# Four-head attention's second head pair added inside the first mixture's first pass, and the joins around the mixture and the entries of the next stages rewritten

## The chip, the cores and the metric

The kernel runs on one core of a Trainium2 chip. The core's engines are TensorE (PE, with its weight loads shown apart as PEld), VectorE (DVE), ScalarE (ACT), GpSimd (POOL) and SyncE (SP), which here only issues transfers. The metric is the time of one execution on the device in microseconds (us), less being better. Everything is computed in float32.

## The reference

The program is a graph network of four layers over 2708 nodes with 256 features, and a 2708 x 2708 adjacency matrix. Each layer adds two results to x, each computed from a layer norm of x. What the change touches, shortened:

```python
# layer 1: attention with 4 heads of 64, then a mixture of 8 experts, top 1
h = (x @ W).reshape(n, 4, 64)
e = leaky_relu(si[:, None, :] + sj[None, :, :], 0.2)      # si, sj: scores of h
att = softmax(where(adj > 0, e, NEG), axis=1)
out = einsum('ijh,jhd->ihd', att, h)

H = gelu(xf @ W1 + b1)                                     # 256 -> 1024
probs = softmax(H @ Wg + bg);  assign = argmax(probs)      # 8 experts
for e in range(8):
    out += where(assign == e, probs[:, e] * (H @ Wd[e] + bd[e]), 0)

# layer 2: attention with one head (Wh = h @ W_w + W_b), then decoder
#          attention and 8 experts (682 hidden, gated), top 2
# layer 3: attention with one head and elu, then a linear layer
```

Layer 0 (a cosine graph attention and a slice attention) is not changed, but for a root that it shares with others. With the reference's inputs the first mixture sends 324, 259, 370, 225, 370, 529, 221 and 410 rows to its eight experts, which fill 25 tiles of 128 rows; the second sends 5416 rows, which fill 47.

## The kernel before

The rows of x stay in on-chip memory as X, 22 tiles of 128 rows (the last has 20). Row tiles are grouped in six blocks of 512 columns (the last has 148). A tile framework gives every instruction its semaphores and sets the order on each engine from the program's order, from when it expects operands to be ready, and from explicit constraints (`issue_after`).

*Four-head attention* (`gat_heads`, from line 762) goes over the heads in two pairs. For each of 22 source tiles j, ScalarE and VectorE form the unnormalised weights e (L668, L669); TensorE multiplies them into six accumulators `acc` of 512 columns (L774), then into `den` (L782), which collects the sums for normalisation. At a pair's end `den` is copied, transposed and inverted (L792 to L800). Then each `acc` is copied to `o`, transposed (L809), multiplied by the reciprocals (L816) and added to X (L823).

*The first mixture* (`top1_ffn`, L850) has two passes. Its eight expert matrices `wd` (8 MB) are loaded on SP's queue (L876), into memory that attention gives back at its end. The statistics for the layer norm follow (L144, L145: sums; L146: a root on ScalarE; L149: its reciprocal on VectorE). The first pass goes over the six blocks: `features` normalises and transposes, `hidden` does 16 matmuls of 512 columns (L905) and a Gelu, `gate` computes the router's logits (L931, L937) and each row's place, and scatters row numbers to lists per expert (L1372); `store` transposes the hidden rows back (L920) and stores them (L924), 512 KB a tile. The order is features of the next block, gate, store.

`route.finish` works out, for every tile of the second pass, which expert it belongs to and where its list starts. The second pass goes over 26 "usual" tiles (a conditional branch, not taken with these inputs, would do more): `fetch` loads a tile's 128 row numbers with a row register on SP (L1474), casts them (L962) and gathers the hidden rows (L964); `transposes` (L978, L979) turns them; `results` does 16 matmul instructions with `wd[expert]`, the expert's number being read to a register of TensorE (L985), and two for the bias `bd` (L988), copies (L992, alternately VectorE and ScalarE) and scatters the rows (L1495). Between the first fetches and the first results stand `route.owners`, `route.weights` and `Head`, which loads the next attention's weights on GpSimd's queue and folds its score vectors into them on VectorE (L651, L654).

*Single-head attention* (`gat_single`, used for layer 2 as g2 and layer 3 as g3) first combines the mixture's rows into X (L1526), takes statistics, normalises (L108), transposes (L1098), and projects (L123) by blocks; `parts` sums the transposed features (L1114); ScalarE makes the exponentials and half of the weighted V (L1111), VectorE the other half (L1113). With a bias, 22 GpSimd additions (L1149) put it into X. The main loop is over destination chunks and 22 source tiles j (L1168).

*The experts of layer 2* (top 2, hidden width 682 in two parts) use the same routing with 47 tiles: `fetch` (L1474, row register), `front` (transposes and place), `hidden` (L1794), `results` (L1826).

Lines of the page, such as L876, are lines of this kernel. What the diff touches:

Of the kernel before, what the change touches and what calls it, by code (L numbers as in the profile page):

```python
# [8 lines left out]
F32 = mybir.dt.float32  # L9
# [21 lines left out]
def slot_tiles(choices, experts=8):  # L31

    return (choices * N + experts * (P - 1)) // P
# [19 lines left out]
class Net:  # L53
# [29 lines left out]
    def load_rows(self, pool, ap, n, name, parts=P):  # L83

        t = pool.tile([parts, n], F32, name=name)
        self.nc.gpsimd.dma_start(t, ap.partition_broadcast(parts))
        return t
# [17 lines left out]
    def normed(self, out, t, ln):  # L105
        mean, rstd = ln
        r = rows(t)
        self.nc.vector.tensor_scalar(  # L108
            out[:r], self.X[:r, t, :], mean[:r, t : t + 1], rstd[:r, t : t + 1], ALU.subtract, ALU.mult
        )  # L110
# [15 lines left out]
class Stats:  # L126
# [9 lines left out]
    def sums(self, t0, t1):  # L136
        net, nc = self.net, self.net.nc
        g = slice(t0, t1)
        if t1 == NT:
            nc.vector.memset(self.mv[:, g, :], 1.0)  # L140
        for t in range(t0, t1):
            r = rows(t)
            st = net.stats.tile([P, 6], F32, name="bnst")
            nc.vector.bn_stats(st[:r], net.X[:r, t, :])  # L144
            nc.vector.bn_aggr(self.mv[:r, t, :], st[:r])  # L145
        nc.scalar.activation(self.sd[:, g], self.mv[:, g, 1], AF.Sqrt, bias=net.ln_eps)  # L146

    def roots(self, t0, t1):
        self.net.nc.vector.reciprocal(self.rstd[:, t0:t1], self.sd[:, t0:t1])  # L149
# [151 lines left out]
def inverse_root(net, pool, v, scale, eps, name):  # L301
# [8 lines left out]
    y = pool.tile([P, n], F32, name=f"{name}y")  # L310
    nc.vector.tensor_scalar(y.bitcast(I32), half, -1.0, float(0x5F3759DF), ALU.mult, ALU.add)
    t = pool.tile([P, n], F32, name=f"{name}t")
    for _ in range(4):
        nc.vector.scalar_tensor_tensor(t, y, -0.5, y, ALU.mult, ALU.mult)
        nc.vector.tensor_tensor(t, t, x, ALU.mult)
        nc.vector.scalar_tensor_tensor(y, t, 1.5, y, ALU.add, ALU.mult)
    return y
# [340 lines left out]
def gat_pairs(net, e, j, i0, iw, big_p, ratio):  # L658
# [10 lines left out]
    nc.vector.scalar_tensor_tensor(v, v, 1.0, net.mask[:, j, i], ALU.add, ALU.mult)  # L669


def gat_heads(net):
# [8 lines left out]
    Q = len(cols) // 2  # L681
    with ExitStack() as ctx:
        big = ctx.enter_context(tc.tile_pool(name="g1big", bufs=1))
        V = big.tile([P, NT, H, DH], F32, name="V")
        ratio = big.tile([P, NT, H], F32, name="ratio")

        low = big.tile([P, NT, H, 2 * Q - 1], F32, name="low")
        big_p = big.tile([P, H, N], F32, name="big_p")
# [73 lines left out]
        for p in range(2):  # L762
# [4 lines left out]
            for j in range(NT):  # L767
# [3 lines left out]
                for n, (i0, iw) in enumerate(cols):  # L771
                    for k, h in enumerate(heads):
                        half = slice(k * DH, (k + 1) * DH)
                        nc.tensor.matmul(  # L774
                            acc[n][half, :iw], V[:, j, h, :], e[:, k, i0 : i0 + iw], start=j == 0, stop=j == NT - 1
                        )
# [13 lines left out]

# [5 lines left out]
            rd = small.tile([P, 4, 4, Q], F32, name="rd", bufs=1)  # L796
# [4 lines left out]
            out = []  # L801
            for n, (i0, iw) in enumerate(cols):
                o = small.tile([P, 512], F32, name="o", bufs=3)
                (nc.vector.tensor_copy if n % 2 else nc.scalar.copy)(o[:, :iw], acc[n][:, :iw])
                pt = paux.tile([P, 4, P], F32, name="aux")
                its = tiles_of(i0, iw)
                for c, i in enumerate(its):
                    r = rows(i)
                    nc.tensor.transpose(pt[:r, c, :], o[:, c * P : c * P + r], net.ident)  # L809
                whole = [c for c, i in enumerate(its) if rows(i) == P]  # L810
                for c0, c1, r in [(0, len(whole), P)] + [(c, c + 1, rows(its[c])) for c in range(len(whole), len(its))]:
                    nt = c1 - c0
                    y = small.tile([P, 4, 2, DH], F32, name="y")

                    d = rd.rearrange("p c (k b) q -> p c k b q", b=2)[:r, c0:c1, :, n // Q, n % Q]
                    nc.vector.tensor_tensor(  # L816
                        y[:r, :nt],
                        pt[:r, c0:c1, :].rearrange("p c (k d) -> p c k d", d=DH),
                        d.unsqueeze(3).to_broadcast([r, nt, 2, DH]),
                        ALU.mult,  # L820
                    )
                    xs = X[:r, its[0] + c0 : its[0] + c1, p * 2 * DH : (p + 1) * 2 * DH]
                    nc.vector.tensor_tensor(xs, xs, y[:r, :nt].rearrange("p c k d -> p c (k d)"), ALU.add)  # L823
# [27 lines left out]
def top1_ffn(net, ctx):  # L851

    nc, tc, a, X = net.nc, net.tc, net.a, net.X
    E, HID = 8, 1024
    KC = HID // P
    with ExitStack() as inner:
        big = ctx.enter_context(tc.tile_pool(name="f1big", bufs=1))
        dram = ctx.enter_context(tc.tile_pool(name="f1dram", bufs=1, space=bass.MemoryType.DRAM))  # L860
        wd = inner.enter_context(tc.tile_pool(name="f1wd", bufs=1, side="right")).tile([P, E, KC, D], F32, name="wd")
# [11 lines left out]
        bd = big.tile([E, D], F32, name="bd")  # L873
        nc.gpsimd.dma_start(bd, a["f1_bd"])
        for e in range(E):
            nc.sync.dma_start(wd[:, e], a["f1_wd"][e].rearrange("(c p) m -> p c m", p=P))  # L876
        route = Routing(net, big, dram, 1, "f")
        ln = net.ln_stats()
# [3 lines left out]
        with tc.tile_pool(name="f1tp", bufs=2, space=PSUM) as ptp, tc.tile_pool(  # L882
# [7 lines left out]
            def features(its):  # L890
                ft = work.tile([P, 2, 512], F32, name="ft")
                for k, t in enumerate(its):
                    r = rows(t)
                    f = rp.tile([P, D], F32, name="f", bufs=2)
                    net.normed(f, t, ln)
# [3 lines left out]

            def hidden(ft, nw):  # L900
                halves = [work.tile([P, KC // 2, 512], F32, name="ht", bufs=3) for _ in range(2)]
# [10 lines left out]
            def store(its, halves):  # L912

                for k, t in enumerate(its):
                    r = rows(t)
                    hr = rp.tile([P, 2, 512], F32, name="hr", bufs=2)
                    for n, half in enumerate(halves):
                        ps = pg.tile([P, 4, P], F32, name=f"hr{n}")
                        for c in range(KC // 2):
                            nc.tensor.transpose(ps[:r, c, :], half[:, c, k * P : k * P + r], net.ident)  # L920
                        (nc.scalar.copy if n else nc.vector.tensor_copy)(
                            hr[:r, n, :], ps[:r].rearrange("p c m -> p (c m)")
                        )
                    nc.sync.dma_start(rows_of[span(t), :], hr[:r].rearrange("p n m -> p (n m)"))  # L924

            def gate(its, halves, nw):
# [5 lines left out]
                q4 = rp.tile([P, 512], F32, name="q4", bufs=1)  # L932
# [9 lines left out]
            blocks = chunks(512)  # L942
            ft = features(tiles_of(*blocks[0]))
            for n, (n0, nw) in enumerate(blocks):
                its = tiles_of(n0, nw)
                halves = hidden(ft, nw)
                if n + 1 < len(blocks):
                    ft = features(tiles_of(*blocks[n + 1]))
                gate(its, halves, nw)
                store(its, halves)  # L950
        route.finish()
        prep = ctx.enter_context(tc.tile_pool(name="g2prep", bufs=1))
        with tc.tile_pool(name="f1t", bufs=1, space=PSUM) as pt, tc.tile_pool(
            name="f1y", bufs=2, space=PSUM
        ) as py, tc.tile_pool(name="f1s", bufs=3) as sp:
            held = {}

            def fetch(s):
                node = sp.tile([P, 1], F32, name="node", bufs=6)
                route.load(s, node)  # L960
                number = sp.tile([P, 1], I32, name="number", bufs=6)
                nc.vector.tensor_copy(number, node)  # L962
                hr = sp.tile([P, 2, 4, P], F32, name="hr", bufs=5)
# [4 lines left out]
                    in_offset=bass.IndirectOffsetOnAxis(ap=number, axis=0),  # L968
                )
                held[s] = hr, node  # L970

            def transposes(s):
                hr, node = held.pop(s)
# [6 lines left out]
                return ht, route.where(sp, s, node)  # L980

            def results(s, ht, to):
                ps = py.tile([P, D], F32, name="y")
                for c in range(KC):
                    nc.tensor.matmul(  # L985
                        ps, ht[:, c // 4, c % 4, :], wd[:, bass.ds(experts[s], 1), c, :], start=c == 0, stop=False
                    )
                last = nc.tensor.matmul(  # L988
                    ps, route.hot[:E, s : s + 1].to_broadcast([E, P]), bd, start=False, stop=True
                )  # L990
                y = sp.tile([P, D], F32, name="ys")
                (nc.scalar.copy if s % 2 else nc.vector.tensor_copy)(y, ps)  # L992
                route.send(to, y)
                return last

            experts = {}

            def through(s0, s1, prepare=None):
                last = None
                for s in range(s0, min(s0 + 4, s1)):  # L1000
                    fetch(s)
                    if prepare and s == s0:
                        route.owners()
                ready = transposes(s0)
                if prepare:
                    prepare()
                for s in range(s0, s1):
                    with tc.issue_after(last.ins) if last else nullcontext():
                        experts[s] = nc.tensor.value_load(route.expert[0:1, s : s + 1], min_val=0, max_val=E - 1)
# [3 lines left out]
                    last = results(s, *this)  # L1013
# [3 lines left out]
            heads = []  # L1017

            def prepare():
                with tc.tile_pool(name="f1wt", bufs=1) as one:  # L1020
                    route.weights(one)
                    heads.append(Head(net, prep, one, "g2", True))

            through(0, route.usual, prepare)
            with route.others():
                through(route.usual, route.tiles)
# [3 lines left out]
class Head:  # L1030


    def __init__(self, net, pool, work, key, bias):
        nc, a = net.nc, net.a

# [1038 lines left out]
```

## Time and profile before

| | |
|---|---|
| median of three runs | 2925.66 us |
| lowest and highest | 2923.8 and 2935.31 us |
| the profiled execution | 2935.18 us |
| its span (first to last instruction) | 2933.1 us |
| busy: PE, PEld | 2676.8 us (91%), 1633.7 us (56%) |
| busy: DVE, ACT, POOL | 1458.5 us (50%), 1046.9 us (36%), 367.2 us (13%) |
| mean granted clock of TensorE | 0.943 of full speed |

The stages, by the times at which TensorE's work changes: four-head attention's two pairs up to 1070; the first mixture's first pass 1096 to 1214; the second pass from 1240 to 1377; attention g2 to 1672; decoder attention and routing to 2200; the experts to 2600; attention g3 from there to 2899; the linear layer to 2933.

In a timeline row the columns are start, length, engine, line, operation, output and inputs, shapes, count, and in brackets the idle time before it with what ended it. In a row of groups, after the bar: busy time of the group and mean nanoseconds of one; after the next bar: idle time of the engine just ahead of them and what ended it. A line "issue" in a chain is time in which the engine waited for nothing that the profile shows.

### The profile page before, as it was taken

How to read it: one execution, taken by the hardware profiler on the slowest of the kernel's cores; microseconds unless marked ns; L12 is line 12 of the kernel's file. 1: busy time of each engine (PE TensorE's matmuls, PEld its weight loads, DVE VectorE, ACT ScalarE, POOL GpSimd, SP SyncE). 2: the span in 40 equal slices, each digit the busy share in tenths (PEclk: the TensorE clock that was granted, in tenths of full speed). 3: DMA queues.
4: the chain of work that ended last, by engine and by line, in shares of the span. 5: the costliest groups of instructions: out<-in, count | busy, mean ns of one | idle time of the engine just before them, and what ended most of it. 6: DMA issues, size and time to landing. Idle time of an engine off the chain costs nothing.

```text
span 2933.1 us, 33103 instructions
## 1 busy us (share of the span) xinstructions
PE 2676.8 (91%) x11945; PEld 1633.7 (56%) x11945; DVE 1458.5 (50%) x3089; ACT 1046.9 (36%) x1605; POOL 367.2 (13%) x464
## 2 busy tenths in 40 slices
PE   6999989799999979797899899999969999969998
PEld 4667646563333325486688433333336676747885
DVE  7743358344777773422644455465543222245455
ACT  3344433225665633211543223233312221224453
POOL 0000012100000001232200123233321111110002
PEclk9999999698999989899999999899959999989999
DMA  8899210000000023443200100002031101041001
GB/s 297 283 293 312 85 64 1 8 0 1 1 1 1 1 85 133 115 130 103 77 1 1 33 22 17 15 2 89 15 109 33 33 30 33 29 151 40 1 1 39
DMA packets 110323, 196.66 MB, mean 67 GB/s; under 512 B 12154, under 2 KB 71034, under 8 KB 107454
## 3 DMA queue, kind: packets, MB, share of 16 engines
q1 hardware_dynamic: 89816, 147.89, 15.6%
q0 software_dynamic: 13360, 38.73, 4.2%
q10 hardware_dynamic: 6986, 7.91, 0.9%
q8 instruction: 100, 1.64, 0.2%
q14 instruction: 61, 0.50, 0.1%
HBM read 134.78 MB, written 59.71 MB: 66 GB/s over the span
## 4 chain that ended last, share of the span: by engine, by line
PE 74%; DVE 10%; DMA 5%; issue 5%; ACT 3%; POOL 2%; ACTq 0%; POOLq 0%; SPq 0%; DVEq 0%
PE acc L1168 15%; PE acc L774 8%; PE acc L278 7%; PE den L782 4%; PE po L1826 4%; PE po L1656 4%; PE sc L1641 3%; PE score L267 3%; DMA f<-hs 3%; PE h L905 3%; PE h L1794 3%; PE pv L123 2%; PE sc L1619 2%; PE po L123 2%; PE y L985 1%
## 5 line engine op out<-in xcount | busy, mean ns | idle before, releaser
L669 DVE SCALAR_TENSOR_TENSOR e<-e,mask 128x768 f32<-128x768 f32 (+2 forms) x264 | 409.5, 1566 | 312.9 <-ACT e L668 312.7
L668 ACT ACTIVATE e<-big_p,minus_one,ratio 128x768 f32<-128x768 f32 (+2 forms) x264 | 394.8, 1513 | 362.8 <-PE acc L1168 229.4
L1168 PE MATMUL acc<-V,e 128*128 128x257 f32 (+1 forms) x1936 | 433.5, 383 | 4.5 <-DVE e L669 2.8
L1168 PEld LDWEIGHTS acc<-V,e 128*128 128x128 f32 (+1 forms) x1936 | 352.2, 186 | 85.8 <-issue 32.1
L774 PE MATMUL acc<-e,V 128*64 128x512 f32 (+1 forms) x1056 | 249.7, 550 | 4.1 <-DVE e L669 4.1
L1794 PE MATMUL h<-w,ft 128*128 x752 | 233.9, 453 | 0.5 <-ACT ft L1783 0.5
L278 PE MATMUL acc<-F,e 128*128 128x257 f32 x968 | 226.3, 384 | 3.0 <-DVE e L275 2.6
L278 PEld LDWEIGHTS acc<-F,e 128*128 128x128 f32 x968 | 173.4, 185 | 67.0 <-DVE e L275 28.4
L774 PEld LDWEIGHTS acc<-e,V 128*64 128x64 f32 x1056 | 95.4, 137 | 180.6 <-issue 158.1
L1641 PE MATMUL sc<-qt,kt 64*128 64x512 f32 (+4 forms) x656 | 185.7, 538 | 4.3 <-ACT e L1651 2.6
L1651 ACT ACTIVATE e<-sc 128x1024 f32<-128x1024 f32 (+4 forms) x140 | 102.7, 760 | 201.1 <-PE sc L1641 177.7
L1794 PEld LDWEIGHTS h<-w,ft 128*128 128x128 f32 x752 | 136.4, 191 | 56.9 <-issue 1.6
L275 DVE TENSOR_TENSOR e<-e,mask 128x512 f32<-128x512 f32 (+2 forms) x132 | 80.5, 625 | 149.2 <-ACT e L269 147.4
L1659 DVE TENSOR_TENSOR sum<-sum,e 128x1024 f32<-128x1024 f32 (+4 forms) x102 | 104.1, 1020 | 97.7 <-ACT e L1651 94.1
L269 ACT ACTIVATE e<-score 128x512 f32<-128x512 f32 (+2 forms) x132 | 69.7, 544 | 179.8 <-PE score L267 153.1
L1656 PE MATMUL po<-e,V 128*64 128x512 f32 (+5 forms) x560 | 119.1, 509 | 14.9 <-ACT e L1651 8.9
L1826 PE MATMUL po<-w,ht 114*128 x564 | 131.2, 382 | 0.9 <-DVE ht L1819 0.9
L1641 PEld LDWEIGHTS sc<-qt,kt 64*128 64x128 f32 x656 | 71.3, 199 | 95.3 <-issue 81.5
L782 PE MATMUL den<-e,low 128*3 128x512 f32 (+1 forms) x1056 | 123.1, 542 | 0.0
L1826 PEld LDWEIGHTS po<-w,ht 114*128 114x128 f32 x564 | 107.9, 191 | 23.1 <-DVE ht L1819 8.2
L1485 DVE TENSOR_SCALAR second<-f,down 128x1 f32<-128x1 f32 x47 | 9.9, 213 | 219.1 <-DMA f<-hs 219.1
L267 PE MATMUL score<-QK 128*128 128x512 f32 (+2 forms) x264 | 112.8, 558 | 1.2 <-ACT e L269 0.7
(600 smaller groups left out, 3554.8 us busy)
## 6 DMA issues: line engine op xcount, KB each, us to landing
row<-in_adj SPq DMA_DIRECT2D x21, 1354.0 KB
raw<-in_adjT SPq DMA_DIRECT2D x35, 768.0 KB
hs<-zero SPq DMA_DIRECT2D x8, 2838.0 KB
hidden<-hr SPq DMA_DIRECT2D x21, 512.0 KB
wd<-in_f_wd SPq DMA_DIRECT2D x8, 1024.0 KB
kept<-mask SPq DMA_DIRECT2D x21, 338.5 KB
mask<-kept SPq DMA_DIRECT2D x21, 338.5 KB
f<-hs SPq DMA_DIRECT2D x47, 129.0 KB
```

The lines of the kernel that those rows point to most:

```text
L123: self.nc.tensor.matmul(out, lhsT[:, c, :], rhs[:, c, :], start=first and c == 0, stop=last and c == n - 1)
L267: nc.tensor.matmul(ps[:r, :iw], QK[:, 0, span(j)], QK[:, 1, i0 : i0 + iw], start=True, stop=True)
L278: nc.tensor.matmul(acc[k][:ri], e[:r, k * P : k * P + ri], F[:r, j, :], start=j == 0, stop=j == NT - 1)
L668: nc.scalar.activation(v, big_p[:, i], AF.Relu, bias=net.minus_one, scale=ratio)
L669: nc.vector.scalar_tensor_tensor(v, v, 1.0, net.mask[:, j, i], ALU.add, ALU.mult)
L774: nc.tensor.matmul(acc[n][half, :iw], V[:, j, h, :], e[:, k, i0 : i0 + iw], start=j == 0, stop=j == NT - 1)
L782: nc.tensor.matmul(den[g : g + Q, :iw], low[:, j, h, Q - 1 - q : 2 * Q - 1 - q], e[:, k, i0 : i0 + iw], start=False, stop=j == NT - 1 and ...
L1168: nc.tensor.matmul(acc[k][:ri], e[:, k * P : k * P + ri], V[:, j, :], start=j == 0, stop=j == NT - 1)
L1641: nc.tensor.matmul(ps[:r, g, o:iw], kt[b, span(j)], qt[b, o:iw], start=True, stop=True)
L1656: nc.tensor.matmul(po[b, o:iw], V[:r, j, g, :], e[:r, g, o:iw], start=j == 0, stop=j == last)
L1794: last = nc.tensor.matmul(halves[s, n][:, q, :HALF], fts[s][:, c, :], weights.w13[n][:, bass.ds(es[s], 1), c, q * HALF : (q + 1) * HALF], ...
L1826: last = nc.tensor.matmul(po, ht[:KP, k, :], w2[:KP, bass.ds(es[s], 1), k, :], start=k == 0, stop=k == KC - 1)
```

## The change

Seven parts, in the order of the program.

1. `gat_heads` does `den` before `acc` for each source tile. Both pairs' `acc` are copied to a buffer `o` that outlives the function; pair 1 is added to X as before; the adding of pair 2 is returned as a function. `top1_ffn` calls it for blocks 0 to 2 ahead of the first hidden rows and for blocks 3 to 5 after block 0's, with the statistics between, in an order on VectorE given by `turn`. For blocks from 1 on, the root is made on VectorE (`newton`). `wd` is loaded after the last add, into the memory of `o`.
2. The hidden rows are stored by half rows (256 KB each) from a buffer of three, which `q4` shares. The store of block 4 follows gate of block 5.
3. The routing gives each expert one of the first eight tiles, so those need no registers; their row numbers come with one transfer (`load_first`). Row numbers, casts and places are kept for all tiles and made in groups of four. Owners and weights come after the first fetch.
4. In the second pass the bias matmul is gone; the copy of each result becomes a VectorE addition of `bd`, held for all partitions (1 MB) and loaded on ScalarE's queue; for tiles from 8 on the expert's number is also read to a register of VectorE. `Head` loads on ScalarE's queue after tile 3.
5. `gat_single` takes `parts` from the copies themselves (`accum_out`, two copies of half the size), leaves the weighted V of blocks 0 to 3 to ScalarE, orders VectorE's steps with `turn`, and uses `newton` for later blocks. The 22 GpSimd additions of the bias come in the first chunk of the main loop, at j = 3.
6. The experts of layer 2 use fixed numbers for their first eight tiles, and `place` is apart from `front`; owners and shares come after the first gate.
7. `inverse_root` does three iterations in place of four.

The core of the diff:

```diff
 def gat_heads(net, keep):
+    o = keep.tile([P, len(cols), 4 * P], F32, name="o")
+    def add(p, n, psum, tag):
+        pt = psum.tile([P, 4, P], F32, name="aux", tag=tag)
+        for c, i in enumerate(its):
+            nc.tensor.transpose(pt[:r, c, :], o[:, n, c * P : c * P + r], net.ident)
+        ...
+            nc.vector.tensor_tensor(y[:r, c0:c1], pt[...], d..., ALU.mult)
+            last = nc.vector.tensor_tensor(xs, xs, y[...], ALU.add)
+        return last
...
             for n, (i0, iw) in enumerate(cols):
+                (nc.vector.tensor_copy if n % 2 else nc.scalar.copy)(o[:, n, :iw], acc[n][:, :iw])
+                if p == 0:
+                    add(p, n, paux, "aux")
+    return lambda n, psum, tag: add(1, n, psum, tag)
...
 def top1_ffn(net, ctx):
+            turn(add, 0, ptp, "tp")
+            turn(stats.sums, *tiles[0])
+            turn(add, 1, ptp, "tp")
+            turn(stats.roots, *tiles[0])
             ft = features(tiles_of(*blocks[0]))
+            turn(stats.sums, *tiles[1], root=False)
+            turn(add, 2, ptp, "tp")
+            turn(stats.sums, *tiles[2], root=False)
+            turn(stats.newton, rp, tiles[1][0], tiles[2][1])
             for n, (n0, nw) in enumerate(blocks):
                 halves = hidden(ft, nw)
                 if n + 1 < len(blocks):
                     ft = features(tiles_of(*blocks[n + 1]))
+                if n == 0:
+                    for m in range(3, len(blocks)):
+                        turn(add, m, ptp, "tp")
+                        turn(stats.sums, *tiles[m], root=False)
+                    turn(stats.newton, rp, tiles[3][0], NT)
+                    held.close()
+                    for e in range(E):
+                        nc.sync.dma_start(wd[:, e], ...)
                 gate(its, halves, nw)
+                kept.append((its, halves))
+                if n + 2 != len(blocks):
+                    for k in kept:
+                        store(*k)
+                    kept.clear()
...
-                last = nc.tensor.matmul(
-                    ps, route.hot[:E, s : s + 1].to_broadcast([E, P]), bd, start=False, stop=True
-                )
-                (nc.scalar.copy if s % 2 else nc.vector.tensor_copy)(y, ps)
+                        e = expert(nc.vector, s)
+                    added = nc.vector.tensor_tensor(y, ps, bd[:, e, :]..., ALU.add)
...
 def gat_single(net, key, head, feed, elu):
-                    nc.scalar.copy(ft[:, :, k * P : k * P + pw], ps[:, :, :pw])
+                    for c in range(2):
+                        nc.scalar.activation(ft[:, c, ...], ps[:, c, :pw], AF.Copy,
+                            accum_out=parts[:, 2 * n + k // 2, c : c + 1])
-                nc.vector.tensor_reduce(parts[:, n, :], ft[:, :, :nw], AX.X, ALU.add)
-            if bias:
-                for t in range(NT):
-                    nc.gpsimd.tensor_tensor(X[:r, t, :], X[:r, t, :], bias[:r], ALU.add)
...
+                if bias is not None and i0 == 0 and j == 3:
+                    for t in range(NT):
+                        nc.gpsimd.tensor_tensor(X[:r, t, :], X[:r, t, :], late[:r], ALU.add)
...
+    def load_first(self, f):
+        self.loaded = self.net.nc.sync.dma_start(
+            f, self.hs.rearrange("(e c) d -> c (e d)", e=self.E)[:P, :]
+        )
```

## The prediction

> **What bounds the kernel now.** I read the chain of work that ended last first, then the engines' busy time stage by stage, then the timeline and the chain inside the stages that the diff touches. The chain, by engine:
>
> ```profile
> PE 74%; DVE 10%; DMA 5%; issue 5%; ACT 3%; POOL 2%; ACTq 0%; POOLq 0%; SPq 0%; DVEq 0%
> ```
>
> TensorE sets the time wherever it has work; what can be won is where it has none. The next view gives, for each stretch, its length, the busy time of PE, PEld, DVE, ACT and POOL, the granted clock, the DMA share and GB/s:
>
> ```profile
> 1070.00:1096.00 26.00, 9.92 (x37) 5.82 (x38) 23.68 (x93) 3.65 (x8) 4.89 (x13) 0.55 0.60 186
> 1096.00:1214.00 118.00, 118.00 (x542) 64.21 (x541) 43.94 (x164) 43.22 (x69) 17.81 (x19) 0.98 0.35 129
> 1214.00:1240.00 26.00, 4.74 (x28) 3.09 (x26) 15.87 (x79) 2.79 (x4) 9.44 (x11) 0.60 0.52 84
> 1302.00:1442.00 140.00, 116.19 (x534) 87.43 (x532) 61.30 (x151) 40.79 (x106) 42.94 (x50) 0.91 0.35 108
> 2165.00:2200.00 35.00, 11.41 (x44) 5.90 (x44) 18.59 (x92) 2.12 (x7) 9.62 (x14) 0.50 0.59 209
> 2590.00:2679.00 89.00, 55.95 (x214) 39.79 (x212) 49.86 (x142) 31.62 (x88) 5.99 (x7) 0.79 0.44 154
> ```
>
> Row 1 is the end of four-head attention: VectorE full, PE a third. Row 2, the first mixture's first pass, is PE without a gap. Rows 3, 5 and 6 are joins (to the second pass, the experts, the last attention) with PE mostly idle; the second half of row 4 is the join to biased attention.
>
> The timeline around row 1 (start, length, engine, line):
>
> ```profile
> 1066.95 2.75 PE L782 MATMUL den<-e,low 128*3 128x512 f32 x24
> ...
> 1083.84 17.83 SPq L876 DMA_DIRECT2D wd<-in_f_wd  x8
> ...
> 1095.55 5.86 PE L905 MATMUL h<-ft,w 128*128 128x512 f32 x8
> ```
>
> Attention's last matmul ends at 1069.70 (call it S); the mixture's first comes at S+25.8. Between lie six adds, all statistics, the first features. The 8 MB of expert weights start meanwhile and keep the rings full for about 25 us.
>
> The chain through row 3, at its DMAs:
>
> ```profile
> 1223.68 4.20 DMA fnodes<-ftag,fto
> ...
> 1229.55 2.71 DMA g2bv<-in_g_b
> ...
> 1236.35 4.04 DMA hr<-hidden,number
> ```
>
> The second is not the mixture's: the folds of the next attention's head, which wait for their own loads, stand on VectorE ahead of the cast of the first tile's numbers.
>
> One steady tile of the second pass, by timeline:
>
> ```profile
> 1346.52 1.09 PE L978 MATMUL ht<-ident,hr 128*128 128x128 f32 x8
> 1347.45 3.62 PE L985 MATMUL y<-wd,ht 128*128 x16
> ...
> 1351.00 0.69 PE L988 MATMUL y<-bd,fhot 8*128 8x256 f32 x2
> 1351.62 1.09 PE L978 MATMUL ht<-ident,hr 128*128 128x128 f32 x8
> ```
>
> 5.10 us from tile to tile, of which the bias matmul is 1351.62 − 1351.00 = 0.62.
>
> Groups of the join to biased attention (busy, mean ns, idle before):
>
> ```profile
> L1149 POOL TENSOR_TENSOR X<-X,g2bv 128x256 f32<-128x256 f32 x21 | 15.5, 770 | 18.9 <-DVE f L108 18.8
> L108 DVE TENSOR_SCALAR f<-X,mv,rstd 128x256 f32<-128x256 f32 x21 | 14.2, 737 | 0.0
> L1114 DVE TENSOR_REDUCE parts<-ft 128x2 f32<-128x1024 f32 x5 | 6.0, 1207 | 4.2 <-ACT ft L1102 4.2
> ```
>
> and the chain into the last one, where ScalarE's root waits until 2626 behind the loads that it waits for in its queue:
>
> ```profile
> 2613.84 11.73 DMA y<-dys
> ...
> 2626.39 1.28 ACT L146
> ```
>
> **What the Trainium skill says.** "SBUF — State Buffer", section on two separate sides: VectorE and GpSimd share a port pair as an exclusive lock. The trace agrees: L108 takes 0.85 in the runs beside L1149 and 0.38 to 0.42 alone. Its section on the DMA setup-cost knee gives 2 us + bytes/436 GB/s: 2.6 us, an estimate, for a 256 KB half-store; no such transfer runs before. "DMA: Bandwidth & Descriptors", Queues, rings and completion order: SP's transfers use one ring on each DMA engine, consumed in order, so a store issued after `wd` waits for it; before shows only `wd`'s 25 us. "TensorE: Matmul & The Clock Gate", Part 1: the clock halves after some 3.4 us idle. Agreed: 8 hidden matmuls take 5.86 us after the gap, 3.44 (8 × 0.43) when warm.
>
> **The change, part by part.**
>
> A, *pair 2 inside the first pass*. Now `den` precedes `acc`, so its copy, transposes and reciprocal hide under the last `acc` matmuls (12 × 0.43 = 5.2 us). From S to the first hidden matmul I count: copy 0.6, four transposes 1.1, multiply and add 1.4, statistics of four tiles 4 × 0.5 = 2.0, table load and root 1.6 (add 1 under it), reciprocal 0.2, features 4 × 1.4 = 5.6: S+12.5 instead of S+25.8, −13.3; `w1` must have landed by then too, about S+11. Against it: the work skipped is not gone. Block 0 gets on VectorE four adds (5 us), 18 tiles' statistics (9), two Newton roots (26 small operations × 0.18 = 4.7), 18.5 in all beside its own 8.8, 27.5 against a block of 22.7: +4.8, and some 0.7 for the strict order, +5.5. `wd` can only load when the buffer `o` is free, about S+43, and four of block 0's eight half-stores are issued behind its 25 us on the same queue; gate's `q4` now shares the three half-row buffers with them. PE has hidden(1) and 12 of 16 rows of hidden(2) ahead (24 us), then a burst of waiting pieces: +5. Ends: −10 (no stall) and +6 (nothing covered). A = −13.3 + 5.5 + 5 ≈ −3.
>
> B, *end of the first pass*. Block 4's store comes after gate(5), so that gate is 3.2 us earlier; the first eight tiles' numbers are one DMA that needs no row register; their cast stands ahead of folds and weights. PE's pause from last gate matmul to first transpose was 1213.16 + 0.98 to 1240.41 = 26.3; I get 23 from the later stores (12 pieces, three buffers held 3.3 us each, paced at 1.1 to 1.25) and the same two DMA landings, with 3 less for the folds. The new loads (1 MB bias rows, head) are on ACT's queue, in the pause. B = −5 (−2 to −9).
>
> C, *second pass*. 26 bias matmuls go, 26 × 0.62 = −16.1. All 26 copies become VectorE adds (L992's copy is 0.42; half of them were on ScalarE), with a register read on 18 dynamic tiles. The trace shows none on VectorE; from below it is nothing, from above I take SP's 1.1 for a row read with its DMA issue. So VectorE has 0.69 + 0.45 + 1.1 = 2.2 per tile, under PE's 4.48. Head folds, 4 us, sit after tile 3's add with 5 us of slack. Uncovered, they would cost their 4. C = −16 (−10 to −17).
>
> D, *join to biased attention*. 22 GpSimd adds leave it for the main loop, whose VectorE does about 1.0 us per source tile against PE's 2.44: hidden; without that cover 16 us. VectorE gains 17 × 0.4 = 7 from f and 6 from L1114, whose sums now ride on two ScalarE copies. ScalarE then has about 6.2 per block against PE's 6.65, so part is lost to bubbles. Main loop from 1441.9 to about 1436: D = −6 (−1 to −9).
>
> E, *experts*. The first eight tiles need no registers: the load goes out at the scatter's landing (2192.94) instead of 2195.06; place, owners and shares come after the first gate. E = −3 (0 to −5).
>
> F, *last join*. ScalarE's wait to 2626 stays. Strict order and Newton roots save some VectorE time after it: F = −4 (0 to −7).
>
> G: one iteration less in the roots, three 0.2 us operations at each of about five calls, partly hidden: −1.
>
> Sum: −3 −5 −16 −6 −3 −4 −1 = −38. Against the profiled execution (span 2933.1, 2.1 us around it, 2935.18) that is 2897; that execution is 9.5 us above the median of the runs shown, 2925.66, so the forecast there is 2888.
>
> **Rivals.** 1: *only C pays*. First pass and joins give back what they gain: ScalarE the bound in D, the `wd` stall at +11. For it: VectorE's 23.68 of 26 in row 1 says that this work moves, not vanishes. Against: row 3's pause has a removable wait. C −16, rest −4: 2906.
> 2: *every join gives its far end*: −10 −9 −17 −9 −5 −5 = −55, 2871. For it: idle PE in all of rows 1, 3, 5, 6. Against: PE restarts at half clock in each.
> 3, the other sign: *three half-row buffers pace the first pass*. Per block eight pieces come in a burst with few hidden matmuls between, so a burst goes at a third of a buffer's hold instead of about 0.9 us a piece. At my 3.3 us hold that is 1.1, about 1.6 a block, in A's range. Loss is 8 × (hold/3 − 0.9) a block over five blocks; to undo 38 and add 15 takes 53, 10.6 a block, hold/3 = 2.2: a hold above 6.7 us decides. For it: stores behind `wd` are held far longer once. Against: before's stores, two whole-tile buffers, left PE 118 busy of 118. It would give about 2941.
> *The change not doing what it says* can be excluded: the counts of tokens per expert fill 25 of the 26 usual tiles, so no extra branch runs.
>
> **How the numbers follow.** Forecast 0.55 (2878 to 2897), rival 1 0.20, rival 2 0.14, rival 3 0.10, the rest 0.01. No change means within 0.5%, 14.6 us, about what a measurement here can tell: 2911 to 2940. Forecast and rival 2 are faster; rival 1 is faster in 0.14 and within in 0.06; rival 3 is slower in 0.09, else within. Faster 0.83, same 0.08, slower 0.09. The range takes in most of rivals 1 and 2 and leaves out rival 3 and rival 2's end: 2862 to 2912.
>
> **What would show it.** A: first hidden matmul 12 to 13 us after attention's last matmul; then a gap of about 5 us near the third block's hidden rows, with `wd` on the queue. B: pause about 23. C: 4.5 us from tile to tile, no bias matmul; a pitch above 5.1 would refute it. D: main loop some 6 us sooner after `fys`, no GpSimd add before it. E: expert PE start 2 to 3 us nearer the scatter. Wrong if the first pass loses more than 10 us or if VectorE's register reads take over 4 us.

## The result, and the profile after

The changed kernel is slower: 2953.18 us, median of 8 runs (2942.62 to 2958.34), against 2924.73 us (2921.38 to 2936.68) before; the ratio is 1.0083, 95% interval 1.0061 to 1.0105. Forecast were 2888 us and a gain. Its profiled execution took 2955.75 us, with a span of 2954.0, 20.9 us above the span of before.

The same stages as in the second view of the prediction, from the view of engine time by stretches (length, busy time of PE, PEld, DVE, ACT, POOL, granted clock, DMA share, GB/s), changed kernel. Here and below a line number is one of the kernel whose run is shown:

```profile
1113.00:1124.00 11.00, 4.65 (x25) 3.10 (x24) 9.77 (x39) 2.17 (x3) 4.46 (x13) 0.78 0.41 107
1124.00:1259.00 135.00, 121.49 (x527) 63.99 (x526) 56.07 (x230) 40.47 (x65) 15.60 (x16) 0.94 0.43 125
1259.00:1295.00 36.00, 10.69 (x58) 6.97 (x56) 14.47 (x67) 5.14 (x8) 9.33 (x10) 0.60 0.61 142
1331.00:1471.00 140.00, 121.20 (x612) 100.36 (x612) 56.67 (x177) 40.03 (x135) 35.51 (x37) 0.94 0.37 117
```

Row 1, the end of attention, has shrunk from 26 to 11 us, much as forecast. But it begins at 1113, not at 1070; the first pass (row 2) is no longer gapless, and the pause after it (row 3) is longer.

Stage by stage, from the starts and ends of TensorE's work in the timelines (a stage reaches from one mark to the next; the last column is the best run below, e12):

| stage | before | after | difference | e12 |
|---|---|---|---|---|
| start to attention's first matmul | 698.55 | 697.39 | -1.2 | 698.79 |
| four-head attention's matmuls | 371.15 | 415.86 | **+44.7** | 366.10 |
| to the first hidden matmul | 25.85 | 11.09 | -14.8 | 11.11 |
| first pass, to its last gate matmul | 118.59 | 134.52 | **+15.9** | 128.21 |
| pause | 26.27 | 36.62 | **+10.4** | 24.25 |
| second pass | 135.96 | 117.30 | -18.7 | 115.44 |
| join to attention g2's main loop | 65.56 | 57.90 | -7.7 | 57.23 |
| main loop, to decoder attention's first matmul | 228.85 | 224.75 | -4.1 | 225.18 |
| decoder attention | 502.93 | 509.55 | +6.6 | 506.74 |
| routing, to the first expert matmul | 26.36 | 22.85 | -3.5 | 22.33 |
| experts | 405.65 | 404.66 | -1.0 | 402.39 |
| join to attention g3's main loop | 73.72 | 67.47 | -6.3 | 66.66 |
| rest | 253.66 | 254.04 | +0.4 | 253.5 |

The sum of the differences is +20.9. Three stages lose 71 us together, and the others win 50. Decoder attention is not touched by the diff: it took 498.3 to 513.2 us in profiles of kernels that have it alike, at a clock of 0.94 in the shortest and 0.91 in the longest, so its +6.6 is no effect of the change.

The largest loss is in attention's loop. First the kernel before, TensorE's timeline (start, length, engine, line, operation; x counts the passes, two for each matmul instruction):

```profile
804.07 2.75 PE L782 MATMUL den<-e,low 128*3 128x512 f32 x24
...
811.46 2.75 PE L782 MATMUL den<-e,low 128*3 128x512 f32 x24
814.14 6.11 PE L774 MATMUL acc<-e,V 128*64 128x512 f32 x24
820.18 2.75 PE L782 MATMUL den<-e,low 128*3 128x512 f32 x24
```

and the changed kernel:

```profile
1047.97 1.03 PE L810 MATMUL den<-e,low 128*3 128x512 f32 x4
1048.93 1.07 PE L821 MATMUL acc<-e,V 128*64 128x512 f32 x2
1049.93 2.74 PE L810 MATMUL den<-e,low 128*3 128x512 f32 x20
1052.60 4.76 PE L821 MATMUL acc<-e,V 128*64 128x512 f32 x22
1057.29 1.03 PE L810 MATMUL den<-e,low 128*3 128x512 f32 x4
```

A source tile now takes 1057.29 - 1047.97 = 9.32 us. Before, two source tiles take 7.39 and 8.72 us in turn, 8.05 on average. With `den` ahead of `acc`, the scheduler starts each source tile with what needs only the first head's e: two `den` and one `acc` instruction. So each run of `den` and each run of `acc` is in two pieces. Four `den` passes take 0.96 us, to the next row's start; the other twenty take 2.67, as long as all twenty-four took before (814.14 - 811.46 = 2.68). No wait stands in these rows.

The second pass by timeline, one tile from L1076 to L1076 (this time from tile to tile is called the pitch below):

```profile
1384.07 3.62 PE L1076 MATMUL y<-wd,ht 128*128 x16
1387.52 1.04 PE L1044 MATMUL ht<-ident,hr 128*128 128x128 f32 x8
1388.40 3.62 PE L1076 MATMUL y<-wd,ht 128*128 x16
```

The pitch is 4.33 us instead of 5.10, forecast 4.5.

### The profile page after: what moved, and what is told of

The parts are those of the page before. It is cut to its first block, busy times and chain, and to the rows that moved or that the text cites. A ratio compares the mean times of both kernels' runs of the same rounds, so it can differ in the third digit from the quotient of the medians.

```text
span 2954.0 us, 32782 instructions
## 1 busy us (share of the span) xinstructions
PE 2703.0 (92%) x11893; PEld 1613.7 (55%) x11893; DVE 1442.7 (49%) x3081; ACT 1039.5 (35%) x1653; POOL 369.2 (12%) x462
## 5 line engine op out<-in xcount | busy, mean ns | idle before, releaser
L675 DVE SCALAR_TENSOR_TENSOR e<-e,mask 128x768 f32<-128x768 f32 (+2 forms) x264 | 411.7, 1574 | 356.7 <-ACT e L674 356.6
L821 PE MATMUL acc<-e,V 128*64 128x512 f32 (+1 forms) x1056 | 256.6, 549 | 0.0
L1919 PE MATMUL h<-w,ft 128*128 (+1 forms) x752 | 234.4, 454 | 0.5 <-ACT ft L1901 0.5
L821 PEld LDWEIGHTS acc<-e,V 128*64 128x64 f32 x1056 | 79.7, 136 | 200.3 <-issue 200.3
L810 PE MATMUL den<-e,low 128*3 128x512 f32 (+1 forms) x1056 | 166.6, 546 | 4.0 <-DVE e L675 4.0
L1951 PE MATMUL po<-w,ht 114*128 (+1 forms) x564 | 129.8, 379 | 0.9 <-DVE ht L1944 0.9
```

The costliest lines, as they stand in the source:

```text
L675: return nc.vector.scalar_tensor_tensor(v, v, 1.0, net.mask[:, j, i], ALU.add, ALU.mult)
L810: nc.tensor.matmul(den[g : g + Q, :iw], low[:, j, h, Q - 1 - q : 2 * Q - 1 - q], e[:, k, i0 : i0 + iw], start=False, stop=j == NT - 1 and ...
L821: nc.tensor.matmul(acc[n][half, :iw], V[:, j, h, :], e[:, k, i0 : i0 + iw], start=j == 0, stop=j == NT - 1)
L1919: last = nc.tensor.matmul(halves[s, n][:, q, :HALF], fts[s][:, c, :], weights.w13[n][:, es[s], c, q * HALF : (q + 1) * HALF], start=c == 0 ...
L1951: last = nc.tensor.matmul(po, ht[:KP, k, :], w2[:KP, es[s], k, :], start=k == 0, stop=k == KC - 1)
```

## The experiments

Ratios are of fresh runs of each kernel to runs of the kernel before on the same chip, with 95% intervals. The chip differs between rows, and the kernel before took 2923.6 to 2928.1 us on them, so the ratios are to be compared, not the times. e1 is made from the kernel before, all others from the changed one.

| run | us | ratio to before |
|---|---|---|
| e1 `den` first, in the kernel before | 2981.11 | 1.0187 (1.0170 to 1.0204) |
| e2 changed, `den` first for the last tile only | 2903.17 | 0.9905 (0.9878 to 0.9932) |
| e5 = e2, weights between stores | 2892.05 | 0.9891 (0.9875 to 0.9908) |
| e6 = e2, store not deferred | 2899.59 | 0.9911 (0.9894 to 0.9927) |
| e7 = e5 and e6 | 2885.88 | 0.9863 (0.9840 to 0.9886) |
| e8 changed, `den` first, order forced | 2905.91 | one run |
| e9 = e7 and e8 | 2881.43 | 0.9834 (0.9821 to 0.9848) |
| e10 = e7, bias by matmul | 2902.54 | 0.9909 (0.9894 to 0.9924) |
| e11 = e7, bias additions early | 2884.99 | 0.9850 (0.9835 to 0.9865) |
| e12 = e9, bias rows loaded later | 2871.98 | 0.9829 (0.9815 to 0.9842) |

**Is it the order of `den` and `acc`?** e1 makes that one edit in the kernel before; e2 takes it back in the changed one for all source tiles but each pair's last, whose early `den` gives the cover that the change wanted.

```diff
 e1, e2 (e2: only for j == NT - 1)
             for j in range(NT):
+                den matmuls (12)
                 acc matmuls (12)
-                den matmuls (12)
```

> Kernel before with one edit: den's matmuls stand ahead of acc's for every source tile. Theory (the new order costs TensorE about 1.0 us in each of 44 source tiles, whatever else is in the change): attention's last matmul ends at about 1113 instead of 1069.7, the time is 2925 + 43 = 2968, ratio 1.015. Rival (attention grew because of the buffer o or the longer first pass): attention ends at 1070 and the time stays at 2925.

> Changed kernel, but den stands ahead of acc only for the last source tile of each pair; acc first for the other 42. Theory: attention ends at about 1070 again, first hidden row still 11 to 12 us later, all else as in the changed kernel: 2953 - 43 = 2910, ratio to before 0.995. Rival (the order is not the cause): 2953.

e1's attention took 418.96 us (371.15 before) and its span is 2978.4. e2's took 369.87, against 415.86 in the changed kernel, and the first hidden row still came 11.1 us later. So the order alone costs 47.8 us in the kernel before and 46.0 in the changed one, net of what it wins at the starts and ends of the pairs, and can be had for the one source tile where it is of use. With this one edit the change is a gain of 0.95%. Its 2903 us are close to rival 1's 2906.

**Why does it cost that?** Either the pieces are dear, or TensorE waits for the second head's e in a way that the rows don't show. e3 and e4 leave out the forming of e for all source tiles but the first of each pair, so TensorE never waits for it, and force TensorE's order. Each was run once.

```diff
 e3: 12 den, 12 acc      e4: 2 den, 1 acc, 10 den, 11 acc
+                if j == 0:
                     e = wide.tile(...); gat_pairs(...) for both heads
+                for step in steps:
+                    with tc.issue_after(last.ins) if last else nullcontext():
+                        last = nc.tensor.matmul(...)
```

> Changed kernel, with e formed for the first source tile of each pair only and used for all 22 (the other 21 formings are left out), so TensorE never waits for it, and TensorE's order forced: 12 den, then 12 acc. Theory (interleaving splits matmuls that run side by side on column groups): the two runs are whole, 7.9 us per source tile (18 slots of 0.43). Rival (den ahead of acc is slow in itself, by the change from one to the other): 9.3 us.

> As the run with one e and whole runs, but in the order that the changed kernel has in its steady state: 2 den, 1 acc, 10 den, 11 acc, so again without any wait for e. Theory (splitting): 21 slots of 0.43, about 9.2 us per source tile. Rival (in the changed kernel TensorE waits for VectorE's second half of e): 7.9 us as in the whole order, since nothing is waited for.

Timeline of e3, whole runs:

```profile
953.24 2.75 PE L816 MATMUL den<-e,low 128*3 128x512 f32 x24
955.92 4.76 PE L828 MATMUL acc<-e,V 128*64 128x512 f32 x24
960.61 2.75 PE L816 MATMUL den<-e,low 128*3 128x512 f32 x24
```

and of e4, split runs:

```profile
957.35 1.03 PE L816 MATMUL den<-e,low 128*3 128x512 f32 x4
958.30 1.07 PE L828 MATMUL acc<-e,V 128*64 128x512 f32 x2
959.31 2.74 PE L816 MATMUL den<-e,low 128*3 128x512 f32 x20
961.98 4.76 PE L828 MATMUL acc<-e,V 128*64 128x512 f32 x22
966.66 1.03 PE L816 MATMUL den<-e,low 128*3 128x512 f32 x4
```

7.37 us against 9.31 for the same 24 instructions on the same data with no wait at all: the split is the cause, and 9.31 is all of the changed kernel's 9.32. (The expected 7.9 was too high, since the sixth block has 148 columns.) The Trainium skill, "TensorE: Matmul & The Clock Gate", Part 3, says that matmuls on different column tiles run at the same time while matmuls start and end strictly in program order. The rows agree: 24 `den` passes, listed at 0.54 us each on average, take 2.7 us; by the code, four instructions in a row write four groups of 32 outputs. When the first two of these stand apart, they run as a pair; the ten left still hold all six instructions of the second head, which use only two of the groups. One `acc` instruction alone leaves half the columns idle. The two splits together cost 1.94 us, 0.97 each.

A split also adds two changes between `den` and `acc` per source tile, and these could be what costs. The rows allow an estimate. A pass of 512 columns takes 0.43 us to the next start (the prediction's 3.44 for 8), an instruction of two passes 0.86. Three full groups of four `den` instructions are then 2.58 us, and took 955.92 - 953.24 = 2.68 in e3, so a change costs some 0.1. The half-filled pair of `den` and the lone `acc` are 2 × 0.86 = 1.72 of the 1.94, and two more changes are the rest.

e8 forces the whole order with e formed as usual:

> The changed kernel with e formed as usual and TensorE's order forced to 12 den, then 12 acc, for every source tile, so that nothing is split but den waits for both halves of e. ScalarE's 2.6 and VectorE's two 3.0 us of e follow the release of a buffer, 8.6 us in all, against the whole order's 7.37 measured without waits. Theory: about 8.6 us per source tile, attention ends near 1080, time about 2920. Rival (splitting only pays because it fills a wait; taken away, the wait is as long): 9.3 us, 2950.

Timeline of e8:

```profile
809.27 2.75 PE L812 MATMUL den<-e,low 128*3 128x512 f32 x24
811.96 4.76 PE L824 MATMUL acc<-e,V 128*64 128x512 f32 x24
816.65 1.03 PE L812 MATMUL den<-e,low 128*3 128x512 f32 x4
817.99 2.74 PE L812 MATMUL den<-e,low 128*3 128x512 f32 x20 [0.31 <-DVE e L675]
820.66 4.76 PE L824 MATMUL acc<-e,V 128*64 128x512 f32 x24
825.35 2.75 PE L812 MATMUL den<-e,low 128*3 128x512 f32 x24
```

Two source tiles take 825.35 - 809.27 = 16.08 us, 8.04 each (7.4 and 8.7 in turn, 7.7 and 8.4 in the second pair), between the 7.37 of no waits and the 8.6 that I had expected from the forming of e. That is the 8.05 of the kernel before: with the runs whole, `den` first costs nothing in the loop. Every second tile is 1.3 us longer, as it waits for VectorE's part of e (L675): a pair of `den` runs alone, and 0.31 us are idle. The order by which the scheduler fills that wait costs 1.94 us in every tile. Attention as a whole took 366.00 us, less than in any order that the scheduler chose; as the loop is no faster than before, the 5.2 us against before and the 3.9 against e2 come from the starts and ends of the pairs.

**The first pass and the pause.** In the changed kernel's timeline the stall stands behind the weights (SPq rows are SP's queue; in brackets the idle time before a row and what ended it):

```profile
1153.03 26.53 SPq L996 DMA_DIRECT2D wd<-in_f_wd  x8
...
1179.66 23.82 SPq L951 DMA_DIRECT2D hidden<-hr  x12
...
1190.01 0.59 ACT L948 COPY hr<-hr 128x512 f32<-128x512 f32 x1 [14.64 <-DMA hidden<-hr]
...
1190.65 1.12 PE L947 MATMUL hr<-ident,ht 128*128 128x128 f32 x4 [8.69 <-ACT hr L948]
```

The first half-store after the weights is issued at 1179.66, when SP has issued the last of them, and the buffer that ScalarE waits for comes free some 10 us later, at 1190.01. The pause stands behind twelve half-stores and then one small load:

```profile
1260.26 20.08 SPq L951 DMA_DIRECT2D hidden<-hr  x12
...
1274.35 0.59 ACT L948 COPY hr<-hr 128x512 f32<-128x512 f32 x1 [7.38 <-DMA hidden<-hr]
...
1282.21 0.41 SPq L1595 DMA_DIRECT2D node<-fnodes  x1
1282.22 0.39 ACTq L1009 DMA_DIRECT2D bd<-in_f_bd  x1
...
1289.42 0.17 DVE L1021 CAST number<-node 128x8 int32<-128x8 f32 x1 [5.91 <-DMA node<-fnodes]
```

The view of waits has what the small load (L1595), which is issued behind the stores on SP, waited for last (us in total, times, longest):

```profile
SPq L1595 <- DMA hidden<-hr: 1.2, 1, 1.2
```

It was the landing of the last half-stores.

e5 spreads the weights, e6 takes the deferral back, e7 does both, each on top of e2.

```diff
 e5, e7: weights
-                    (n == 0) for e in range(E): nc.sync.dma_start(wd[:, e], ...)
+                after the stores of block n:
+                for e in range(2 * n, min(2 * n + 2, E)): nc.sync.dma_start(wd[:, e], ...)
 e6, e7: store
-                if n + 2 != len(blocks):
-                    for k in kept: store(*k)
-                    kept.clear()
+                for k in kept: store(*k)
+                kept.clear()
```

> The changed kernel with den first only for the last source tile, and the eight expert weight loads spread over the first four blocks, two after each block's stores, instead of all eight ahead of block 0's last stores. Theory (half-stores wait behind 8 MB on SP's queue): the first pass falls from 134.2 to about 122 us, the pause after it stays at 36.8, time about 2891. Rival (three half-row buffers pace the first pass whatever is ahead of them): it stays above 130 us and the time within 4 us of 2903.

> The changed kernel with den first only for the last source tile, and block 4's store ahead of gate 5 again, weights loaded together as in the change. Theory (twelve half-stores after the last gate matmul, paced by three buffers, hold up VectorE's steps of the routing behind their copies): the pause falls from 36.8 to about 25 us, the first pass grows by 3 to 5, time about 2895. Rival (the pause is long because of the one transfer of row numbers or the loads on ScalarE's queue): it stays at 36 us.

> Both: den first only for the last source tile, weight loads spread over four blocks, block 4's store not deferred. If the two stalls are separate the gains add: first pass about 125 us, pause about 25, time about 2883, ratio to before 0.985. If they are one chain (buffers late from the first stall on), the gain is that of the larger alone, about 2891.

First pass and pause: e2 134.18 and 36.80, e5 125.70 and 35.83, e6 138.81 and 26.92, e7 129.48 and 27.04. So the weights' place costs 8.5 us in the first pass, and the deferral 9.9 in the pause, for 4.6 won in the pass. Each is read from one profile. Stages that kernels have alike differ between profiles: with the weights together and the store deferred (changed kernel, e2, e3, e4, e8) the first pass took 132.4 to 134.7 us and the pause 35.8 to 36.8; with both taken back the first pass took 128.2 to 132.4 us (e7, e9 to e12) and the pause 25.8 to 27.6 (e7, e9, e11, which have the same loads in it). So both effects are clear, but their sizes are no surer than these 2 to 4 us. By the times of whole runs neither e5 nor e6 can be told from e2, as the intervals overlap, and e7's only just touches e2's. The two add, within that: 134.18 + 36.80 - 129.48 - 27.04 = 14.5, against 9.5 + 5.3 = 14.8 from the parts. My rival of the buffers pacing the whole pass falls, since e5 recovers half of its loss. They pace the tail: in the pause of the changed kernel the copies into them wait 10.8 us on ScalarE and 7.3 on VectorE for stores to land.

Even so e7's end of attention, pass and pause take 11.09 + 129.48 + 27.04 = 167.6 us against 170.7 before, about as long. The 14.8 us won ahead of the pass are lost again in it: in a stretch of 130.00 us around e7's first pass TensorE is busy for 124.25, so idle for 5.7, and 2.2 us are pair 2's moved transposes. The rest of the 10.9 that e7's pass is longer than before was not taken apart.

**The bounds of what was won.** e9 is the sum of e7 and e8. e10 and e11 take back one part each from e7.

```diff
 e10
-                    added = nc.vector.tensor_tensor(y, ps, bd[:, e, :]..., ALU.add)
+                    last = nc.tensor.matmul(ps, route.hot[...], bd, start=False, stop=True)
+                    added = (nc.scalar.copy if s % 2 else nc.vector.tensor_copy)(y, ps)
 e11
+            for t in range(NT): nc.gpsimd.tensor_tensor(X[:r, t, :], X[:r, t, :], bias[:r], ALU.add)
-            (the same additions in the main loop at j == 3)
```

> The run with both stalls mended, and TensorE's order in attention forced to 12 den, then 12 acc. Expected: attention 366.0 instead of 369.9 us as in the run with the forced order alone, all else the same, about 2882, ratio to before 0.985. Rival (the forced order takes e's slack, so that a later start of ScalarE at the pair's end eats the gain): 2886.

> The run with both stalls mended, and the bias of the second pass by matmul again, with the copies alternating between VectorE and ScalarE. Theory (the tile's pitch is TensorE's; the matmul and its change of shape cost 0.77 us): pitch back from 4.33 to 5.10 us, second pass 115 + 20 = 135, time about 2905. Rival (part of the gain is from the fixed first eight tiles and the earlier row numbers): second pass 125 to 130.

> The run with both stalls mended, and the 22 GpSimd additions of the bias ahead of biased attention's main loop again. Theory (they share a port with VectorE and slow the normalisation from 0.4 to 0.85 us a tile): the join, 57.1 us, grows by 4 to 7, time about 2891. Rival (the VectorE order set by the change leaves it slack, ScalarE bounds the blocks): it grows by less than 1.

e9: attention 366.07, and 0.9834; the intervals of e7 and e9 overlap, so the gain over e7 is shown by the stage alone. e10: the second pass is 136.72 us instead of 114.94 and the pitch 5.10 again (1314.68 to 1319.78), so the whole gain of that stage is the bias's. It also showed something unforeseen: the pause fell from 27.04 to 22.07, where the bias rows are 8 KB instead of 1 MB. e11: the join is 57.28 us against 57.07, no change. Yet in the groups of e11's join (busy, mean ns of one, idle before) the normalisation is slow again:

```profile
L1258 POOL TENSOR_TENSOR X<-X,g2bv 128x256 f32<-128x256 f32 (+1 forms) x22 | 16.5, 780 | 22.8 <-DVE f L108 22.8
L108 DVE TENSOR_SCALAR f<-X,mv,rstd 128x256 f32<-128x256 f32 (+1 forms) x22 | 13.3, 668 | 0.2
```

668 ns a tile, near the 737 of before, where e7 has 408. VectorE has that to spare in the join as it is now, so moving the additions won nothing.

e12 follows up on e10: the bias rows go behind the first four gathers.

```diff
-            nc.scalar.dma_start(bd..., a["f1_bd"]...partition_broadcast(P))
             for s in range(4):
-                fetch(s)
+                got = fetch(s)
+            with tc.issue_after(got.ins):
+                nc.gpsimd.dma_start(bd..., a["f1_bd"]...partition_broadcast(P))
```

> The run with both stalls mended and the whole order, and the 1 MB of bias rows loaded on GpSimd's queue behind the first four gathers instead of on ScalarE's queue beside the first row numbers. Theory (the small transfer of row numbers, 4 KB, takes 6.7 us from issue to cast because 1.6 MB goes with it, against 2.5 us where the bias rows were 8 KB): pause from 25.8 to about 22, and the second pass unchanged at 116, time about 2878. Rival (the bias rows then come late for the first tile's addition, and delay the next gathers): the pause falls but the second pass grows by as much, 2881.

Timeline of e12:

```profile
1218.37 0.41 SPq L1598 DMA_DIRECT2D node<-fnodes  x1
...
1222.46 0.17 DVE L1022 CAST number<-node 128x8 int32<-128x8 f32 x1 [2.94 <-DMA node<-fnodes]
```

From issue to cast 4.1 us, where the changed kernel had 7.2, e7 6.7 and e10 2.5. The pause is 24.25 against e9's 25.82, and the second pass is not longer. By times the step from e9 to e12 cannot be told from none: the intervals, 0.9821 to 0.9848 and 0.9815 to 0.9842, overlap. Both beat the kernel before and the changed kernel.

## Why the prediction was wrong, step by step

- **A, the order of `den`.** This is the step that failed. "Now `den` precedes `acc`, so its copy, transposes and reciprocal hide under the last `acc` matmuls" counted what the new order gives once per pair and nothing for what it does in the 44 source tiles of both pairs. There the scheduler splits both runs, and a source tile takes 9.32 us instead of 8.05; net of what is won at the starts and ends of the pairs, attention is 44.7 us longer, more than the 38 forecast as the whole gain. e3 and e4 show the split as the cause, e8 that the order without it costs nothing in the loop. I had the order of the instructions on TensorE before me and read it for the joins alone. The rows of before held the sign too: 24 passes listed at 0.54 us each in 2.75 us say that something runs side by side that can be pulled apart.
- **A, first hidden matmul.** 11.1 us after attention's end, forecast 12.5: right.
- **A, first pass.** Forecast +10.5, measured +15.9. The weights' stall was the right mechanism (block 0's half-stores behind 8 MB on SP's queue, though they are already held at their issue, until 1179.66) but cost 8.5, not 5: TensorE ran out of work at 1182.0, waited 8.7 us in one piece and then went on in short ones.
- **B, the pause.** Forecast 23, measured 36.6. The step that failed is "12 pieces, three buffers held 3.3 us each, paced at 1.1 to 1.25", 13 to 15 us: the twelve stores took 20.1 us to issue. The copies into free buffers stand on VectorE and ScalarE among the routing's own steps, and each held the other up; above all, the load of the row numbers stands behind the stores on SP and went out only at 1282.21, when the last had landed. The deferral is worth -5.3 us when taken back. The loads "on ACT's queue, in the pause", costed at nothing, hold the row numbers up by 4 us (6.7 from issue to cast in e7, 2.5 in e10).
- **C, second pass.** -18.7, and -21.8 by e10 against e7, forecast -16: mechanism right, size low. Leaving the matmul saves 0.77 a tile, not the 0.62 that its own rows show, because the next transposes start 0.10 and the next matmuls 0.05 us sooner after what precedes them. VectorE's register reads did not show in the pitch.
- **D, join to biased attention.** -7.7, forecast -6: size right, reason wrong. e11 shows that the GpSimd additions don't matter there. What remains, the strict VectorE order, the `accum_out` copies and the roots by `newton`, was not told apart. (Beside the additions L108 mostly takes 0.80 to 0.83 us, not the 0.85 that I had read.)
- **E and F.** -3.5 and -6.3, forecast -3 and -4: right. **G** can't be told from the rest; the 4.1 us won ahead of decoder attention may be part of it.
- **The rivals.** Rival 3 named the right buffers, but put them in the wrong place: they paced the tail of the first pass, and not all of it, and by far less than the 53 us that it needed. Rival 1 had half of it: the first pass gives back what is won ahead of it, but the joins (-7.7, -3.5, -6.3) do not. None of the rivals was in attention's main loop, so the range had no room for what happened.
- **Sums.** Two were off and decided nothing: the 18.5 us of VectorE work in A add up to 18.7, and B's terms, a gate 3.2 us earlier and a pause 3.3 us shorter, to 6.5, where 5 was put down with no reason given.

## What to carry to other kernels

If an edit reorders matmuls in a loop, multiply by the loop and see which instructions stand next to each other in the schedule: matmuls on part of the columns gain only from neighbours on the other part, and a scheduler that fills a wait with what is ready can undo the pairing at a higher price than the wait. An order that is needed at a loop's end can be had in its last turn alone. Spread a large load between the small stores of the same queue, and keep large loads off the moment at which a small one is waited for; of these two, only the stages above show the gain, not the whole time.

## What was not expected of the hardware

- Splitting a run of column-tiled matmuls in two cost about 0.97 us per split (9.31 against 7.37 us for two), with no wait and the same instructions.
- A 4 KB load of row numbers on SP's queue took 7.2 us to its use beside 1.4 MB of loads issued just after it on ScalarE's queue, 4.1 beside 0.4 MB (e12), 2.5 beside the 8 KB of bias rows alone (e10). "DMA: Bandwidth & Descriptors", Queues, rings and completion order, says that the engines take turns between the queues packet by packet; here this did not keep a small transfer short.
